# Graph layer, attention and a mixture of experts on one core: the experts' first layer in seven products for eight

## The chip, the core and the metric

The kernel runs on one core of a Trainium2 chip. TensorE multiplies matrices into eight banks of PSUM; VectorE, ScalarE and GpSimd do the rest of the arithmetic; SyncE (SP) and GpSimd issue the transfers. Each engine works through its own instructions in their order, and semaphores order the engines among each other. The metric is the device time of one execution in microseconds (us). Before the change the median of three runs is 1558.56 us (1558.55 to 1558.76).

## The reference

`x` is 4096 tokens of 256 numbers, `adj` a 4096 x 4096 matrix of weights. All is float32.

```
f = layernorm(x)
x = x + concat(f, adj @ (f @ neigh_W.T) / (adj.sum(1) + 1)) @ lin_W.T
z = layernorm(x)                      # then a transformer block on z
z1 = z + attention(rmsnorm(z)) @ wo.T           # causal, 4 heads, 2 of keys
flat = rmsnorm(z1)
weights = the two largest of softmax(flat @ router_w.T), normalised
for e in range(8):                              # the experts
    hh = silu(flat @ w1[e].T) * (flat @ w3[e].T)        # 682 wide
    out = out + weights[:, e:e+1] * (hh @ w2[e].T)
result = x + z1 + out
```

Only an expert's own tokens (two experts for each token) have weights that aren't zero, so the kernel computes only those.

## The kernel before

The program has three stages on one core. The first (to about 533 us) is the product with `adj`, in seven products for eight (Strassen's scheme in Winograd's form: 2 x 2 blocks, sums of blocks ahead, sums of products behind). The second (to about 1044 us) is the attention; while it runs, each token's row is scattered into the lists of its two experts in memory. The third, from 1044 us on, is the experts, and the change lies in it.

**Groups.** An expert's list is cut into groups of 256 rows (whole groups, numbers 0 to 24) and a rest in groups of 128 rows (small groups, 25 to 41; 42 to 45 are rare and run only if the lists need them). `TURNS` gives the order: a place k in it (0 to 41) has group `TURNS[k]`. Places 0 to 8 are whole groups; after them small and whole ones are mixed by their share, and the last `LAST` places are whole groups.

**One group.** `load13` brings w1 and w3 of the group's expert (128 x 2 x 1408 numbers; blocks of 128 outputs, w1 and w3 in turn, and a last block that holds the 42 left-over rows of both), `load2` brings w2, `load_rows` the rows. Weights have five buffers, so they come four to five places ahead. `prepare` transposes the rows on TensorE into a bank and ScalarE copies them, scaled, to `xT`. `hidden` (L1457) is the first layer: for each pair of blocks, 128 x 128 weights stay in the array and 256 (small group: 128) columns of `xT` pass, two products for the two halves of the 256 inputs (L1476); ScalarE takes silu of one bank (L1482) and VectorE multiplies it with the other bank (L1483). These banks come from three pools of two banks each in turn (`p_sc`). `combine` is the second layer. For a small group it is six products with 256 columns (L1528) into a bank `y`, which VectorE scales (L1543). For whole groups from place 4 on (`SEVEN`) it is seven products for eight: `split` (L1412 to L1419) has VectorE make eight sums of 128 x 384, `seven_products` (L1440) fills banks `y` and `ms`, VectorE adds the products up (L1447 to L1454) and ScalarE scales (L1539). Each half of a group is then scattered by GpSimd with addition into a buffer in memory (L1548).

**The order.** The order of all instructions is written by hand. For place k it is: `hidden(k)`, in it `prepare(k+1)` and at its end `split(k)`; the load of w13 for place k+5; `combine(k-1)`; the loads of rows and w2 for place k+4. So TensorE does a first layer, the transposes for the next group, then the second layer of the group before. VectorE has `split(k)` ahead of the scaling of place k-1, and that ahead of the multiplications of place k+1. `load_rows(k+4)` on SyncE waits until the scatter of place k-1 has landed, as it overwrites the row numbers that the scatter uses.

**The end.** Scatters of all but the last `LAST` groups add into `acc_dram`. Then one transfer copies that to the output (L1671), and the last groups' scatters add into the output itself, so they wait for the copy.

Of the kernel before, what the change touches and what calls it, by code (L numbers as in the profile page):

```python
# [9 lines left out]
F32 = mybir.dt.float32  # L10
I32 = mybir.dt.int32
SP = mybir.EngineType.SP
AF = mybir.ActivationFunctionType
ALU = mybir.AluOpType
# [3 lines left out]
P = 128  # L18
# [30 lines left out]


ALONE = 9
LAST = 5
RARE = 4
NM = NG - RARE
TURNS = list(range(ALONE)) + [
# [10 lines left out]
def fast_kernel(  # L66
# [596 lines left out]
    with (  # L663
# [1 line left out]
        tc.tile_pool(name="eg", bufs=1) as eg,  # L665
        tc.tile_pool(name="ex", bufs=2) as ex,
        tc.tile_pool(name="ax", bufs=2) as ax,
        tc.tile_pool(name="a_sc0", bufs=1, space=PSUM) as p_sc0,
        tc.tile_pool(name="a_sc1", bufs=2, space=PSUM) as p_sc1,
        tc.tile_pool(name="a_sc2", bufs=1, space=PSUM) as p_sc2,  # L670
        tc.tile_pool(name="a_y", bufs=1, space=PSUM) as p_y,
        tc.tile_pool(name="a_ms", bufs=1, space=PSUM) as p_ms,
    ):

        HALF = GR // P
        pt_all = sp.tile([P, 9 * 1024], F32, name="pt_all")
# [25 lines left out]
            given_back.update(keys)  # L702
            ring[:] = [r for r in ring if homes.get(id(r)) not in given_back]

        p_sc = cycle((p_sc0, p_sc2, p_sc1))
        p_sa = cycle((p_sc0, p_sc2))
        y_banks = [
            pool.tile([P, 512], F32, tag=tag, name=name) for pool, tag, name in (
# [662 lines left out]
        def prepare(k, pool=p_y, tag="y"):  # L1371
            i = TURNS[k]
            n = halves(i)
            tr = pool.tile([P, 2, n, P], F32, tag=tag, name=f"tx_{i}")
            for h in range(n):
                for c in range(2):
                    nc.tensor.transpose(  # L1377
                        tr[:, c, h, :], rows[i][:, h, c * P : (c + 1) * P], ident
                    )
            xT = late[:, LATE_XT + k % 2 * 2 * GR : LATE_XT + k % 2 * 2 * GR + 2 * n * P]  # L1380
            xT = xT.rearrange("p (c i) -> p c i", c=2)
            for c in range(2):
                nc.scalar.activation(  # L1383
                    xT[:, c, :], tr[:, c].rearrange("p h i -> p (h i)"), AF.Copy,
                    scale=ln2_sb[:, c : c + 1],
                )
            inputs_of[i] = xT

        SEVEN = [k for k in range(4, NM - 2) if TURNS[k] < NW]
        parts_of = {}

        def split(k, hT):

# [60 lines left out]
        def hidden(k, step=None, behind=None):  # L1457
# [4 lines left out]
            free_bank = k >= SEVEN[0]  # L1462

            for q in range(0, NF + 1, 2):
                pool = next(p_sc)
                if pool is p_sc1:
                    ps = [
                        pool.tile([P, 2, GR], F32, tag="sc", name=f"h_{i}_{q}_{m}")[:, :, 0:n]
                        for m in range(2)
                    ]  # L1470
                else:
                    ps = pool.tile([P, 2, 2, GR], F32, tag="sc", name=f"h_{i}_{q}")
                    ps = [ps[:, m, :, 0:n] for m in range(2)]
                for m in range(2 * q, min(2 * q + 4, 2 * NF + 1)):
                    for c in range(2):
                        nc.tensor.matmul(  # L1476
# [169 lines left out]
        def step():  # L1646
            for f in next(rest, []):
                f()

        load13(2)  # L1650
        load2(2)
        load13(3)
# [2 lines left out]
        for k in range(NM):  # L1655
            if k == NM - 1:


                between = iter([lambda: None, lambda: combine(k - 1)])
            hidden(  # L1660
                k, step if k < NM - 1 else lambda: next(between)(),
                k + 1 if k + 1 < NM else None,
            )
            step()
            if k + 5 < NM:
                load13(k + 5)
            if 0 < k < NM - 1:
                combine(k - 1)
                step()
            if k == NM - LAST:  # L1670
                nc.sync.dma_start(out, acc_dram[0:N, :])  # L1671
            if k + 4 < NM:
                load_rows(k + 4)
            if k + 4 < NM:
                load2(k + 4)
        combine(NM - 1)
    kv_scope.close()
    return lists

# [736 lines left out]
```

## Time and profile before

| | |
|---|---|
| median of three runs | 1558.56 us |
| profiled execution | 1558.78 us |
| its span | 1557.0 us |
| granted TensorE clock, mean | 0.999 |

The profile is of one execution, so its durations add up to 1558.78 us: the span and 1.8 us around it. Busy time by stage, from the trace (us):

| stretch | long | TensorE | VectorE | ScalarE | GpSimd | memory, GB/s |
|---|---|---|---|---|---|---|
| 0 to 533.4, product with `adj` | 533.4 | 528.1 | 379.6 | 53.5 | 290.2 | 140 |
| to 1043.7, attention | 510.3 | 509.0 | 418.6 | 302.3 | 235.1 | 37 |
| to 1187.7, places 0 to 9 | 144.0 | 144.0 | 83.2 | 38.7 | 43.4 | 240 |
| to 1472.1, whole and small groups mixed | 284.4 | 284.4 | 129.2 | 75.9 | 64.0 | 246 |
| to 1550, the last five first layers | 77.9 | 76.5 | 34.9 | 17.8 | 21.4 | 146 |

Lines of the profile have a start (or a total), a duration, the engine, the line of the code and what was written from what. PE is TensorE, PEld its loads of weights, DVE VectorE, ACT ScalarE, POOL GpSimd, SP SyncE. A float32 product of the program is two matrix instructions in the trace, so the 22 products of a first layer are x44. Matrix instructions overlap: the time that one takes in the stream is the distance of the starts, not the duration shown. In brackets stands how long the engine sat idle before, and what ended it.

### The profile page before, as it was taken

The numbers are of one execution on the slowest core, as the hardware profiler recorded it, in microseconds if no ns is written. First come the engines' busy times: TensorE is split into PE (matmuls) and PEld (weight loads), VectorE is DVE, ScalarE is ACT, GpSimd is POOL, SyncE is SP. The second block draws the span as 40 slices with busy tenths as digits, with TensorE's granted clock in tenths as the row PEclk, the third lists the DMA queues.
The fourth block names the chain that finished last, engine by engine and source line by source line (L and its number), as shares of the span: only waits on it lengthen the run. The fifth ranks groups of instructions, "written<-read, shape, count | busy, mean of one in ns | idle before, by whom it ended". The sixth has DMA issues, their size and how long they took to land.

```text
span 1557.0 us, 27444 instructions
## 1 busy us (share of the span) xinstructions
PE 1541.9 (99%) x10692; PEld 1133.8 (73%) x10692; DVE 1045.4 (67%) x2137; ACT 488.1 (31%) x884; POOL 655.0 (42%) x725
## 2 busy tenths in 40 slices
PE   8999999999999999999999999999999999999997
PEld 7888888888888643444444444358899999999996
DVE  7966677766766677779879878785565453544462
ACT  1101010010010356555665655652122222222221
POOL 3446557565565323364564553442422212122213
PEclk9999999999999999999999999999999999999999
DMA  6344444443444000011011011048677778777772
GB/s 236 129 129 146 139 139 135 139 139 136 139 136 142 32 1 16 29 36 51 29 57 33 29 39 37 22 184 314 192 229 207 228 249 264 232 242 246 237 232 29
DMA packets 68507, 209.34 MB, mean 134 GB/s; under 512 B 17488, under 2 KB 45520, under 8 KB 54736
## 3 DMA queue, kind: packets, MB, share of 16 engines
q1 hardware_dynamic: 55104, 189.50, 35.5%
q0 software_dynamic: 12720, 17.47, 5.8%
q8 instruction: 86, 1.41, 0.4%
q10 hardware_dynamic: 544, 0.52, 0.1%
q14 instruction: 53, 0.43, 0.1%
HBM read 184.48 MB, written 27.13 MB: 136 GB/s over the span
## 4 chain that ended last, share of the span: by engine, by line
PE 96%; DVE 2%; DMA 0%; POOL 0%; issue 0%; ACT 0%; SPq 0%; POOLq 0%; DVEq 0%; ACTq 0%
PE acc L493 25%; PE h L1476 21%; PE sc L757 14%; PE y_first L799 5%; PE y_second L799 5%; PE ye_y L1528 4%; PE y_third L799 4%; PE ye_y L1440 3%; PE ye_ms L1440 2%; PE pq L194 2%; PE ph L545 2%; PE pf L464 1%; PE po L876 1%; PE tx L1377 1%; PE trq L229 1%; PE tr L376 1%
## 5 line engine op out<-in xcount | busy, mean ns | idle before, releaser
L757 PE MATMUL sc<-qT_all,kT 64*64 64x512 f32 (+3 forms) x2304 | 282.0, 557 | 1.0 <-ACT pt_all L765 0.5
L493 PE MATMUL acc<-a,g 128*128 128x256 f32 x1024 | 245.9, 380 | 0.0
L1548 POOL DMA_INDIRECT acc_dram<-y,late x57 | 89.8, 1575 | 334.9 <-DVE y L1543 185.5
L493 PEld LDWEIGHTS acc<-a,g 128*128 128x128 f32 x1024 | 193.0, 190 | 31.6 <-DVE vv L511 1.2
L757 PEld LDWEIGHTS sc<-qT_all,kT 64*64 64x64 f32 x2304 | 91.2, 133 | 130.1 <-issue 108.2
L1483 DVE TENSOR_TENSOR late<-si,h 128x256 f32<-128x256 f32 (+2 forms) x126 | 62.7, 506 | 183.0 <-ACT si L1482 180.2
L765 ACT ACTIVATE pt_all<-sc 128x1024 f32<-128x1024 f32 (+3 forms) x157 | 149.0, 956 | 95.7 <-PE sc L757 95.1
L448 POOL TENSOR_TENSOR all_s<-all_s,more_sums 128x512 f32<-128x512 f32 x72 | 106.4, 1491 | 106.0 <-DVE more_sums L440 106.0
L1476 PE MATMUL h<-late,qT_all 128*128 128x256 f32 (+1 forms) x792 | 147.2, 345 | 0.0
L1482 ACT ACTIVATE si<-h 128x256 f32<-128x256 f32 (+2 forms) x126 | 57.0, 453 | 276.6 <-PE h L1476 269.4
L1476 PEld LDWEIGHTS h<-late,qT_all 128*128 128x128 f32 x792 | 130.1, 191 | 15.2 <-ACT late L1383 0.8
L493 PE MATMUL acc<-more_sums,g 128*128 128x256 f32 x512 | 126.2, 379 | 0.0
L785 DVE TENSOR_TENSOR late<-late,pt_all 128x1024 f32<-128x1024 f32 (+3 forms) x92 | 107.7, 1171 | 23.0 <-ACT pt_all L765 9.6
L1476 PE MATMUL h<-late,pt_all 128*128 128x128 f32 (+1 forms) x704 | 113.5, 321 | 0.0
L1476 PEld LDWEIGHTS h<-late,pt_all 128*128 128x128 f32 x704 | 103.5, 191 | 8.0
L493 PEld LDWEIGHTS acc<-more_sums,g 128*128 128x128 f32 x512 | 97.2, 190 | 14.8
L799 PE MATMUL y_second<-pt_all,vv 64*64 64x512 f32 (+3 forms) x440 | 105.0, 555 | 0.0
L799 PE MATMUL y_first<-pt_all,vv 64*64 64x512 f32 (+3 forms) x440 | 104.3, 553 | 0.0
L1035 POOL DMA_INDIRECT lists<-row,slots x64 | 90.2, 1410 | 18.0 <-issue 15.3
L799 PE MATMUL y_third<-pt_all,vv 64*64 64x512 f32 (+3 forms) x376 | 89.8, 557 | 0.0
L378 ACT COPY qT_all<-tr 128x512 f32<-128x512 f32 x30 | 16.2, 589 | 210.5 <-PE tr L376 210.4
L1476 PE MATMUL h<-late,res_all 128*128 128x256 f32 (+1 forms) x352 | 68.3, 353 | 0.0
(394 smaller groups left out, 2997.4 us busy)
## 6 DMA issues: line engine op xcount, KB each, us to landing
a<-in_adj_dram SPq DMA_DIRECT2D x64, 1024.0 KB
qT_all<-in_w_dram SPq DMA_DIRECT2D x18, 1408.0 KB
pt_all<-in_w_dram SPq DMA_DIRECT2D x16, 1408.0 KB
res_all<-in_w_dram SPq DMA_DIRECT2D x17, 768.0 KB
pt_all<-in_w_dram SPq DMA_DIRECT2D x16, 768.0 KB
res_all<-in_w_dram SPq DMA_DIRECT2D x8, 1408.0 KB
qT_all<-in_w_dram SPq DMA_DIRECT2D x9, 768.0 KB
late<-lists SPq DMA_DIRECT2D x25, 265.0 KB
```

The source lines that it names most:

```text
L448: nc.gpsimd.tensor_add(all_s[:, i], all_s[:, i], sums_at[n % 2][k])
L493: nc.tensor.matmul(acc[bank][:, at, :], g[jb][:, right, k, :], m[left][:, k, :], start=(jb == 0 and k == 0 and at == 0), stop=(jb == NB - ...
L757: nc.tensor.matmul(ps[k * HP : (k + 1) * HP, j, :w], kT[sb][hd, i * P + k * HP : i * P + (k + 1) * HP], qT[b][hd, p, off:], start=True, st ...
L765: nc.scalar.activation(pt[:, :, :w], ps[:, :, :w], AF.Exp, scale=HD ** -0.5)
L785: nc.vector.tensor_add(sums[b, p][:, :, off:], before[:, :, off:], pt[:, :, : 512 - off])
L799: nc.tensor.matmul(accs[b, p][k][hd, off:], vv[sb][some, i, hd], pt[some, j, : 512 - off], start=(s == order_of(b)[0]), stop=(s == order_o ...
L1035: put = nc.gpsimd.indirect_dma_start(out=lists[:, :], out_offset=bass.IndirectOffsetOnAxis(ap=chosen[b][:, k, t, :], axis=0), in_=flats[b] ...
L1440: nc.tensor.matmul(p[number], m[left][:, j, :], m[right][:, j, :], start=(n % 4 == 0 and j == 0), stop=(j == 2), skip_group_check=True,)
L1476: nc.tensor.matmul(ps[m % 2][:, m // 2 - q, :], w13_sb[:, c, m * P : (m + 1) * P], xT[:, c, :], start=(c == 0), stop=(c == 1),)
L1483: nc.vector.tensor_mul(hT[:, q : q + both, :], si[:, 0:both, :], ps[1][:, 0:both, :])
L1528: nc.tensor.matmul(ps[h if last else 0][:, h, :], hT[:, q, cols], w2_sb[:, q, :], start=(q == 0), stop=(q == NF),)
L1548: put = nc.gpsimd.indirect_dma_start(out=(acc_dram if k < NM - LAST else out)[:, :], out_offset=at, in_=y[:, h, :], in_offset=None, comput ...
```

## The change

- `LAST` goes from 5 to 3. Places 9 to 38 now have small and whole groups in turn (at three of them two small ones follow each other), and only the last three places are whole groups in a row. The copy to the output starts two places later.
- 14 whole groups, at the places 10, 12, 14, 17, 19, 21, 23, 26, 28, 30, 33, 35, 37 and 39 (`SPLIT13`), get their first layer in seven products for eight. The 2 x 2 blocks are w1 or w3 against the two halves of the inputs, and the two halves of the inputs against the two halves of the 256 rows. A block product is five products of 128 x 128 by 128 columns, one for each block of outputs. The tail (the last block) stays as it was.
- The four sums of the weights (128 x 640 each) are made by GpSimd (`sums13`), two places ahead, just after `hidden(k)` in the program and ahead of `combine(k-1)`'s scatter. The four sums of the inputs are made by VectorE at the end of `prepare` (`sums_x`), from the bank with the transposes.
- `hidden_seven` replaces `hidden` in these groups. It works in two parts, of four and of one block of outputs, each with three banks (A, D, B). Products are collected in the banks; between them ScalarE copies bank A (`s1`, `u2`) and bank D (`s5`) out, VectorE adds later banks to the copies, ScalarE takes silu of `s1` and `u2` in SBUF, and VectorE multiplies `u2` with `s5` and `s1` with the last bank A.
- The three pools of two banks are closed after the attention, and one pool of six single banks (`e_h`) is opened for all first layers. The plain `hidden` takes two of them a step.

```diff
--- before.py
+++ after.py
@@ -49,7 +49,7 @@
 ALONE = 9
-LAST = 5
+LAST = 3
 RARE = 4
 NM = NG - RARE
 TURNS = list(range(ALONE)) + [
@@ -665,12 +665,14 @@
         tc.tile_pool(name="eg", bufs=1) as eg,
         tc.tile_pool(name="ex", bufs=2) as ex,
         tc.tile_pool(name="ax", bufs=2) as ax,
-        tc.tile_pool(name="a_sc0", bufs=1, space=PSUM) as p_sc0,
-        tc.tile_pool(name="a_sc1", bufs=2, space=PSUM) as p_sc1,
-        tc.tile_pool(name="a_sc2", bufs=1, space=PSUM) as p_sc2,
         tc.tile_pool(name="a_y", bufs=1, space=PSUM) as p_y,
         tc.tile_pool(name="a_ms", bufs=1, space=PSUM) as p_ms,
     ):
+        sc_scope, ctx_h = ExitStack(), ExitStack()
+        p_sc0, p_sc1, p_sc2 = (
+            sc_scope.enter_context(tc.tile_pool(name=f"a_sc{n}", bufs=bufs, space=PSUM))
+            for n, bufs in ((0, 1), (1, 2), (2, 1))
+        )
         HALF = GR // P
         pt_all = sp.tile([P, 9 * 1024], F32, name="pt_all")
@@ -702,7 +704,6 @@
             given_back.update(keys)
             ring[:] = [r for r in ring if homes.get(id(r)) not in given_back]
-        p_sc = cycle((p_sc0, p_sc2, p_sc1))
         p_sa = cycle((p_sc0, p_sc2))
         y_banks = [
             pool.tile([P, 512], F32, tag=tag, name=name) for pool, tag, name in (
@@ -1385,12 +1386,172 @@
                     scale=ln2_sb[:, c : c + 1],
                 )
             inputs_of[i] = xT
+            if k in SPLIT13:
+                sums_x(k, tr)
         SEVEN = [k for k in range(4, NM - 2) if TURNS[k] < NW]
-        parts_of = {}
+        SPLIT13 = [k for k in SEVEN if k > ALONE]
+        parts_of, sums13_of = {}, {}
+        p_h = []
+        rooms13 = [
+            room.rearrange("p (s k i) -> p s k i", s=3, k=NF)
+            for room in (
+                sum_all[:, 0 : 3 * NF * P],
+                res_all[:, 2 * W13 + 2 * W2 : 2 * W13 + 2 * W2 + 3 * NF * P],
+            )
+        ]
+        def sums13(k):
+            if k not in SPLIT13:
+                return
+            chunks = w13s[k % 5][:, :, 0 : 2 * NF * P].rearrange(
+                "p c (k r i) -> p c r k i", r=2, i=P
+            )
+            m = {f"A{r + 1}{c + 1}": chunks[:, c, r] for r in range(2) for c in range(2)}
+            for n, name in enumerate(("S1", "S2", "S4")):
+                m[name] = rooms13[SPLIT13.index(k) % 2][:, n]
+            m["S3"] = m["A21"]
+            nc.gpsimd.tensor_add(m["S1"], m["A21"], m["A22"])
+            nc.gpsimd.tensor_sub(m["S2"], m["S1"], m["A11"])
+            nc.gpsimd.tensor_sub(m["S4"], m["A12"], m["S2"])
+            nc.gpsimd.tensor_sub(m["S3"], m["A11"], m["A21"])
+            sums13_of[k] = m
+        def sums_x(k, tr):
+            xT = inputs_of[TURNS[k]]
+            room = kT[6 + SPLIT13.index(k) % 2].rearrange("p (n i) -> p n i", n=4)
+            m = {f"T{n + 1}": room[:, n] for n in range(4)}
+            for c in range(2):
+                for h in range(2):
+                    m[f"B{c + 1}{h + 1}"] = xT[:, c, h * P : (h + 1) * P]
+            for dst, c, h, less in (
+                ("T1", 0, 1, "B11"), ("T2", 1, 1, "T1"), ("T3", 1, 1, "B12"), ("T4", 1, 0, "T2"),
+            ):
+                nc.vector.scalar_tensor_tensor(
+                    m[dst], tr[:, c, h, :], ln2_sb[:, c : c + 1], m[less],
+                    op0=ALU.mult, op1=ALU.subtract,
+                )
+            sums13_of[k].update(m)
+        def hidden_seven(k, step, behind):
+            i = TURNS[k]
+            m, xT, w13_sb = sums13_of.pop(k), inputs_of.pop(i), w13s[k % 5]
+            hT = hTs[k % 2]
+            room_x = (
+                qT_all[:, 2 * (2 * W13) + W2 :] if SPLIT13.index(k) % 2
+                else wqkv_sb.rearrange("p c w -> p (c w)")[:, 0:1024]
+            )
+            room_y = ax.tile([P, TB, ROW], F32, tag="row", name=f"hy_{i}")
+            room_y = room_y.rearrange("p t c -> p (t c)")
+            room_z = ax.tile([P, 512], F32, tag="yT0", name=f"hz_{i}")
+            class Part:
+                pass
+            parts = []
+            for n, (k0, k1) in enumerate(((0, NF - 1), (NF - 1, NF))):
+                q = Part()
+                q.chunks = range(k0, k1)
+                q.rows = slice(k0, k1)
+                q.A, q.D, q.B = (
+                    p_h[0].tile([P, 4, P], F32, tag="h", name=f"h{name}_{i}_{n}")
+                    for name in "ADB"
+                )
+                w = (k1 - k0) * P
+                rooms = (
+                    [room_x[:, 0:w], room_x[:, w : 2 * w], room_y[:, 0:w]]
+                    if n == 0 else [room_z[:, j * w : (j + 1) * w] for j in range(3)]
+                )
+                q.s1, q.u2, q.s5 = (
+                    r.rearrange("p (k i) -> p k i", i=P) for r in rooms
+                )
+                q.pair = (room_x if n == 0 else room_z)[:, 0 : 2 * w]
+                parts.append(q)
+            one, two = parts
+            def product(q, bank, left, right, first=False):
+                for n, c in enumerate(q.chunks):
+                    nc.tensor.matmul(
+                        bank[:, n, :], m[left][:, c, :], m[right],
+                        start=first and n == 0, stop=True, skip_group_check=True,
+                    )
+            def copied(dst, q, bank):
+                nc.scalar.copy(dst, bank[:, 0 : len(q.chunks), :])
+            def added(dst, q, bank):
+                nc.vector.tensor_add(dst, dst, bank[:, 0 : len(q.chunks), :])
+            def begun(q):
+                product(q, q.A, "A11", "B11", True)
+                copied(q.s1, q, q.A)
+                product(q, q.D, "S1", "T1", True)
+                copied(q.s5, q, q.D)
+                product(q, q.B, "A12", "B21", True)
+            def second(q):
+                product(q, q.A, "S2", "T2")
+                copied(q.u2, q, q.A)
+                product(q, q.D, "S4", "B22")
+            def added_up(q):
+                added(q.s1, q, q.B)
+                added(q.u2, q, q.D)
+            def third(q):
+                product(q, q.A, "S3", "T3")
+                added(q.s5, q, q.A)
+            def gated(q):
+                nc.scalar.activation(q.pair, q.pair, AF.Silu)
+            def last(q):
+                product(q, q.A, "A22", "T4")
+            def multiplied(q):
+                nc.vector.tensor_mul(hT[:, q.rows, P:GR], q.u2, q.s5)
+                nc.vector.tensor_mul(
+                    hT[:, q.rows, 0:P], q.s1, q.A[:, 0 : len(q.chunks), :]
+                )
+            begun(one)
+            second(one)
+            added_up(one)
+            step()
+            begun(two)
+            tail = two.B[:, 2:4, :].rearrange("p k i -> p (k i)")
+            for c in range(2):
+                nc.tensor.matmul(
+                    tail, w13_sb[:, c, 2 * NF * P :], xT[:, c, :],
+                    start=False, stop=(c == 1), skip_group_check=True,
+                )
+            second(two)
+            added_up(two)
+            gated(one)
+            third(one)
+            third(two)
+            step()
+            if behind is not None:
+                prepare(behind, p_ms, "ms")
+            gated(two)
+            si = ax.tile([P, GR], F32, tag="rden", name=f"si_{i}_t")
+            nc.scalar.activation(si[T0 : T0 + TAIL, :], tail[0:TAIL, :], AF.Silu)
+            last(one)
+            last(two)
+            multiplied(one)
+            multiplied(two)
+            nc.vector.tensor_mul(
+                hT[T0 : T0 + TAIL, NF, :], si[T0 : T0 + TAIL, :], tail[T0 : T0 + TAIL, :]
+            )
+            hidden_of[i] = hT
+            split(k, hT)
         def split(k, hT):
@@ -1462,15 +1623,10 @@
             free_bank = k >= SEVEN[0]
             for q in range(0, NF + 1, 2):
-                pool = next(p_sc)
-                if pool is p_sc1:
-                    ps = [
-                        pool.tile([P, 2, GR], F32, tag="sc", name=f"h_{i}_{q}_{m}")[:, :, 0:n]
-                        for m in range(2)
-                    ]
-                else:
-                    ps = pool.tile([P, 2, 2, GR], F32, tag="sc", name=f"h_{i}_{q}")
-                    ps = [ps[:, m, :, 0:n] for m in range(2)]
+                ps = [
+                    p_h[0].tile([P, 2, GR], F32, tag="h", name=f"h_{i}_{q}_{m}")[:, :, 0:n]
+                    for m in range(2)
+                ]
                 for m in range(2 * q, min(2 * q + 4, 2 * NF + 1)):
                     for c in range(2):
                         nc.tensor.matmul(
@@ -1647,6 +1803,8 @@
             for f in next(rest, []):
                 f()
+        sc_scope.close()
+        p_h.append(ctx_h.enter_context(tc.tile_pool(name="e_h", bufs=6, space=PSUM)))
         load13(2)
         load2(2)
         load13(3)
@@ -1657,11 +1815,15 @@
                 between = iter([lambda: None, lambda: combine(k - 1)])
-            hidden(
-                k, step if k < NM - 1 else lambda: next(between)(),
-                k + 1 if k + 1 < NM else None,
-            )
+            if k in SPLIT13:
+                hidden_seven(k, step, k + 1)
+            else:
+                hidden(
+                    k, step if k < NM - 1 else lambda: next(between)(),
+                    k + 1 if k + 1 < NM else None,
+                )
             step()
+            sums13(k + 2)
             if k + 5 < NM:
                 load13(k + 5)
             if 0 < k < NM - 1:
@@ -1674,6 +1836,7 @@
             if k + 4 < NM:
                 load2(k + 4)
         combine(NM - 1)
+        ctx_h.close()
     kv_scope.close()
     return lists
```

## The prediction

> **What bounds it now.** I read the page's busy shares and its chain of work that ended last, then that chain from 1290 to 1345 us, then the timeline of all engines there, then the first stage for what GpSimd does to VectorE.
>
> ```profile
> PE 1541.9 (99%) x10692; PEld 1133.8 (73%) x10692; DVE 1045.4 (67%) x2137; ACT 488.1 (31%) x884; POOL 655.0 (42%) x725
> ...
> PE 96%; DVE 2%; DMA 0%; POOL 0%; issue 0%; ACT 0%; SPq 0%; POOLq 0%; DVEq 0%; ACTq 0%
> ```
>
> TensorE sets the end; the other engines have room. In the chain, a whole group (x44 at 9.50) and a small one (x44 at 4.91) follow each other without a gap:
>
> ```profile
> 1305.01 4.91 PE h L1476 x44
> 1309.92 0.44 PE tx L1377 x4
> 1310.36 2.68 PE ye_y L1440 x24
> 1313.04 2.01 PE ye_ms L1440 x18
> 1315.05 9.50 PE h L1476 x44
> 1324.55 0.22 PE tx L1377 x2
> 1324.77 2.59 PE ye_y L1528 x12
> 1327.36 4.91 PE h L1476 x44
> ```
>
> So a change gains what it takes from TensorE's stream and loses every wait that it puts into it. The timeline shows the waits that are now just covered:
>
> ```profile
> 1303.56 0.56 DVE L1412 TENSOR_TENSOR kT<-late 128x384 f32<-128x384 f32 x1
> ...
> 1308.44 0.48 DVE L1543 TENSOR_SCALAR y<-ye_y,gt 128x256 f32<-128x256 f32 x1
> ...
> 1310.19 1.50 PE L1440 MATMUL ye_y<-qT_all,late 128*128 128x128 f32 x12
> ...
> 1315.09 0.29 DVE L1451 TENSOR_TENSOR vv<-vv,ye_ms 128x128 f32<-128x128 f32 x1 [0.78 <-PE ye_ms L1440]
> ...
> 1315.73 1.03 ACT L1539 ACTIVATE y<-vv,gt 128x256 f32<-128x256 f32 x2 [2.39 <-DVE vv L1452]
> ...
> 1318.39 1.57 POOL L1548 DMA_INDIRECT acc_dram<-y,late  x1 [0.19 <-issue]
> ```
>
> VectorE frees bank y at 1308.92, TensorE writes it again at 1310.19: 1.27 us of slack. L1451 starts 0.21 after TensorE's last product at 1314.88: that is TensorE to VectorE. ScalarE to TensorE is 0.06 (its L765 ends 535.63, sc goes on at 535.69), VectorE to TensorE 0.10 (first L174 done at 549.80, transposes at 549.90).
>
> **The products.** One product is two instructions. 44 long ones run from 1314.88 to 1324.38, 0.2159 each; 44 short ones from 1327.19 to 1332.11, and the 42 of L1440 in 4.69, 0.1117 each. Of a whole group's 44 long ones 40 go (8.64 us) and 70 short ones come (7.82); the tail's 4 stay (0.86). Saved: 0.82 a group, 14 groups, **-11.4 us**. The ratio 0.1117 : 0.2159 is 0.52, under the 4 : 7 at which seven for eight breaks even.
>
> [...] L1440's 42 back-to-back instructions decide for 0.1117.
>
> **The new chain in a whole group.** I set t = 0 at its first product and lay the new order out; a short product is 0.223. First and second round of the four-chunk part end at 4.46, the one-chunk part's first at 5.13, the tail at 6.00, its second at 6.44, the third round at 7.34 and 7.56, transposes of the small group behind (x2, 0.22) at 7.78. Each product into a used bank waits for its reader. The copies (128x512, 0.59 as L378; 128x128, 0.27 as L1447) are queued on ScalarE behind L1539 of the group before, which ends at t = 1.88: they end at 2.47 and 3.06, where TensorE wants the banks at 2.68 and 3.57. Covered, by 0.15 in the first case; if the cover went, 0.1 to 0.3 a group.
>
> Not covered is the last product, A22 T4, which adds to bank A after VectorE has read the third round from it: 7.34 + 0.21 + 0.69 (128x512 with one input in a bank, as L1483) + 0.10 = 8.34, against 7.78. **A wait of 0.56 in 13 groups; 0.34 in the last**, with four transposes behind: +7.6 us. Bounds: 0.4 to 0.7 each. The last products end at 9.45 instead of 9.72.
>
> **GpSimd's sums.** Four of 128x640. By L448 (512 wide, 1.26) and L453 (256 wide, 0.73) one is 1.53, four 6.1; bounds 1.45 to 1.8 each, as these are strided and depend on one another. Their data is early: that weight load was issued over 20 us before. In GpSimd's queue they stand behind the two scatters of the group before last (the second at 1318.39, done by t = 5.1) and ahead of the next scatter, whose y comes at t = 16 or later: it isn't delayed, nor SyncE's loads that wait for it. But GpSimd holds VectorE:
>
> ```profile
> 78.68 1.58 POOL L448 TENSOR_TENSOR all_s<-all_s,more_sums 128x512 f32<-128x512 f32 x1 [5.85 <-DVE more_sums L440]
> 79.73 0.69 DVE L469 TENSOR_TENSOR res_all<-res_all,pf 128x512 f32<-128x512 f32 x1 [0.60 <-PE pf L464]
> ```
> ```profile
> 112.26 1.26 POOL L448 TENSOR_TENSOR all_s<-all_s,qT_all 128x512 f32<-128x512 f32 x1
> 112.39 0.36 DVE L161 BATCH_NORM_AGGREGATE mv<-st 128x2 f32<-128x6 f32 x4
> 112.67 1.40 DVE L438 TENSOR_TENSOR more_sums<-a 128x512 f32<-128x512 f32 x1
> ```
>
> L469, one input in a bank, keeps its 0.69. L438, both in SBUF, takes 1.40 instead of 0.69: it ends 0.55 after the GpSimd operation. At a boundary of two such operations VectorE gets in and GpSimd waits (the pair at 117.35 takes 3.01, not 2.5).
>
> The sums run from t = 5.1: 6.7, 8.2, 9.7, 11.3. The adds from banks pass. The product of gate and copy (u2 with s5, both in SBUF) is due at 8.56, its silu long done (128x1024, 1.02 as L765, from 6.7), and is held to 9.7, done 10.3, and pushes the fourth sum to 11.8; its one-chunk twin is held to that, done 11.9; then 0.3 and 0.42 (tail): the split starts at 12.7 instead of 11.15 (now 11.0). Split 4.46 and y's 0.90 by the rows: bank y free at 18.08 (without the hold 16.55). TensorE wants it at 9.45 + 2.59 + 4.91 + 0.44 = 17.39. With the 0.10, **a new wait of 0.79**; without the hold none. VectorE's four sums of the inputs (0.29 each as L1448) then end level with the need for bank ms: 0.1 more. This happens where the group two before is whole and the one two after is one of the 14: places 10, 12, 19, 21, 28, 35, 37, seven times: +6.2 us. Elsewhere the sums fall earlier or there are none. Bounds: 0 (VectorE slips through) to 1.5 each.
>
> **The end.** The copy of the sums to the output now starts two groups later, behind the scatter of place 38. From the first product of place 39: y at 16.55, scatter 0.29 on, copy 6.23 after it (1488.75 to 1494.98), so 23.1. By its row (first scatter behind it 1511.11) it holds GpSimd for 16.1, to 39.2. Of the six scatters then left the last starts 2.1 + 4 x 1.87 later (as from 1511.11 and 1518.24), at 48.8. TensorE alone would set it to 9.45 + 2.59 + 9.94 + 4.69 + 19.87 (place 41 with its two second layers) + 0.96 to the scatter (1548.40 to 1549.36), 47.5: +1.3. Bounds: 0 (the copy shares the queues with no load now) to 2.7 (y's buffer waits for place 39's scatters to land).
>
> Six banks in a row instead of three pools: a hidden layer still gets each bank back after three steps, now in halves. The first ones take over banks that the unload leaves at 1046.48, wanted at 1048.76: nothing; if all six waited for that, 2.8. VectorE's and ScalarE's added work has room apart from the waits named.
>
> **Sum:** -11.4 + 7.6 + 6.2 + 1.3 = +3.7 on 1558.8; the median is 0.2 lower: **1562.3**. A difference under 0.2% (3.1 us) can't be told from none.
>
> **Rivals.**
> - As forecast, 1559.5 to 1566: 44%. Some two thirds of it is slower by over 0.2%.
> - GpSimd's sums don't reach TensorE: -11.4 + 7.6 and 0 to 1.3 for the end, 1555 to 1556. Not slower. It decides from the point where VectorE loses under 0.7 us a group to the sums: bank y's slack of 17.39 - 16.55. For it: only two of VectorE's operations before the split have both inputs in SBUF. Against it: 112.67. 24%.
> - The wait before the last product is hidden too: 1547 to 1552. It takes a read of bank A done in 0.4 us, which no row shows. 13%.
> - The sums are slower (1.8 and more each), or two waits push one another on: 7 x 1.5 and a wait of 0.7, 1567 to 1575. 19%.
> - Short products that are no cheaper: no room for it beside L1440's rows.
>
> The range takes in all but the best of the third and the worst of the fourth: 1551 to 1570. Faster by over 0.2%: all of the third (13%) and 13 of the second's 24; within: the other 11 of it and 15 of the first's 44, 26%; slower: 29 of the first and all of the fourth, 48%.
>
> **What would show it.** Right: in a whole group 70 short instructions in 7.8 us; TensorE idle some 0.5 us before the last round, released by VectorE's add; idle again before the seven products of the second layer in seven groups, released by L1543's like; VectorE's SBUF product at over 1 us beside GpSimd's sums. Wrong: no idle in TensorE's row, or idle at the first copies, at the inputs' sums, or where the stages meet.

## The result and the profile after

The changed kernel takes 1571.49 us (median of 6 runs, 1568.12 to 1574.74) beside 1558.55 of the kernel before on the same chip (6 runs, 1558.19 to 1558.76). The ratio is 1.0083, with a 95% interval of 1.007 to 1.0096: slower by some 13 us, where 3.7 had been forecast. The runs of the kernel before lie within 0.6 us, those after within 6.6. The profiled execution took 1571.55, with a span of 1569.7 (before: 1558.78 and 1557.0), so 12.7 us of span are to be found.

The page's busy shares and the shares of its chain by engine come first.

```profile
PE 1541.1 (98%) x11112; PEld 1141.3 (73%) x11112; DVE 1116.1 (71%) x2291; ACT 516.9 (33%) x954; POOL 746.4 (48%) x781
...
PE 87%; DVE 9%; ACT 1%; issue 1%; DMA 1%; POOL 1%; SPq 0%; DVEq 0%; ACTq 0%; POOLq 0%
```

VectorE now holds 9% of the chain, 2% before, so new waits lie on the path. TensorE counts as busy as long as before (1541.1 beside 1541.9), though 14 x 0.82 us of products went: the lengths of its instructions cover part of a wait (below, a wait that costs 0.60 is listed with 0.34), and some ran at a clock of 0.50 (1047.97 to 1051.39, below). The list of what TensorE waited for (total, times, longest) names them. None of these lines is in the list of the kernel before.

```profile
PE hA L1481 <- DVE hy L1490: 4.5, 13, 0.4
PE h L1632 <- DVE yT L809: 2.8, 1, 2.8
PE ye_ms L1601 <- DVE pick L1664: 2.5, 8, 0.8
...
PE ye_y L1601 <- DVE y L1699: 1.2, 3, 0.4
PE sc L758 <- DVE res_all L552: 1.1, 1, 1.1
```

The first line is the wait that the prediction priced. The second and fifth lie where the stages meet, where it priced nothing and which it had named as a sign of being wrong. The third is for bank ms, the fourth for bank y; the prediction had put nearly all of the sums' loss on bank y.

To see what each costs, I cut both traces at the same places: the experts' first product, the start of place 10 (the first group in seven products), the end of TensorE's last product, and the end of the span.

| us | before | after | difference |
|---|---|---|---|
| start to the experts' first product | 1043.67 | 1047.11 | +3.44 |
| from there to place 10 | 144.03 | 147.54 | +3.51 |
| place 10 to TensorE's end | 360.86 | 364.39 | +3.53 |
| TensorE's end to the end of the span | 8.44 | 10.66 | +2.22 |

The four add up to 12.7. More than half lies ahead of place 10, before any product of the new kind runs. The timeline around the experts' first product shows the first row:

```profile
1044.70 1.75 DVE L786 TENSOR_TENSOR sum_all<-sum_all,res_all 128x256 f32<-128x256 f32 x2
1046.38 0.68 DVE L809 TENSOR_TENSOR yT<-yT,y_second 128x512 f32<-128x512 f32 x1
1047.11 5.41 PE L1632 MATMUL h<-late,qT_all 128*128 128x256 f32 x16 [2.80 <-DVE yT L809]
```

TensorE stands still for 2.8 us until VectorE has read the last values from y_second. The sixteen instructions behind take 5.41 us where sixteen of 0.2159 take 3.5. The stretches of half a microsecond say why; the third number from the end is the granted clock (then follow the DMA share and GB/s):

```profile
1047.50:1048.00 0.50, 0.50 (x4) 0.45 (x3) 0.00 (x0) 0.50 (x1) 0.00 (x0) 0.97 0.95 356
1048.00:1048.50 0.50, 0.50 (x3) 0.41 (x2) 0.00 (x0) 0.41 (x1) 0.00 (x0) 0.50 1.03 387
...
1051.00:1051.50 0.50, 0.50 (x3) 0.38 (x3) 0.00 (x0) 0.00 (x0) 0.00 (x0) 0.61 1.13 457
1051.50:1052.00 0.50, 0.50 (x4) 0.45 (x3) 0.00 (x0) 0.31 (x1) 0.00 (x0) 1.00 1.03 427
```

By the means of the first and third of these stretches the clock is at 0.50 from 1047.97 to 1051.39: 3.42 us at half speed, 1.7 us lost. The rest of the second row (1.8) is at places 8 and 9, where the first sums on GpSimd run.

In a whole group the chain of waits now reads like this, in the stretch that the prediction showed for the kernel before:

```profile
1301.24 0.70 DVE hy L1490
1301.98 1.17 PE hA L1481 x8
1303.18 0.69 DVE late L1520
...
1304.96 1.14 DVE kT L1573
...
1313.11 0.87 DVE kT L1436 x3
1314.12 2.25 PE ye_ms L1601 x18
```

VectorE's add of the third round (L1490) stands ahead of the last products, as forecast. Then the chain stays on VectorE: gate by value and the split (its first operation at 1.14 where 0.56 is its length without company). From 1310.51 it passes VectorE's first multiplication of the small group, two silu and the copies of the inputs on ScalarE, and goes back to VectorE for the sums of the inputs from bank ms; the second layer gets bank ms 0.14 us after the last of them.

### The profile page after: what moved, and what is told of

Its sections match the earlier page's. It is cut to its first block, busy times and chain, and to the rows that moved or that the text cites. A ratio compares the mean times of both kernels' runs of the same rounds, so it can differ in the third digit from the quotient of the medians.

```text
span 1569.7 us, 28703 instructions
## 1 busy us (share of the span) xinstructions
PE 1541.1 (98%) x11112; PEld 1141.3 (73%) x11112; DVE 1116.1 (71%) x2291; ACT 516.9 (33%) x954; POOL 746.4 (48%) x781
## 4 chain that ended last, share of the span: by engine, by line
PE 87%; DVE 9%; ACT 1%; issue 1%; DMA 1%; POOL 1%; SPq 0%; DVEq 0%; ACTq 0%; POOLq 0%
PE acc L493 24%; PE sc L758 14%; PE h L1632 10%; PE y_second L800 5%; PE y_third L800 4%; PE y_first L800 4%; PE hA L1481 4%; PE ye_y L1684 3%; PE ye_ms L1601 2%; PE pq L194 2%; PE hD L1481 2%; PE ph L545 2%; DVE sum_all L786 1%; PE po L877 1%; PE ye_y L1601 1%; PE pf L464 1%
## 5 line engine op out<-in xcount | busy, mean ns | idle before, releaser
L1704 POOL DMA_INDIRECT acc_dram<-y,late x61 | 95.6, 1568 | 275.7 <-DVE y L1699 167.0
L1638 ACT ACTIVATE si<-h 128x256 f32<-128x256 f32 (+2 forms) x84 | 34.9, 417 | 204.2 <-PE h L1632 182.1
L1632 PE MATMUL h<-late,qT_all 128*128 128x128 f32 (+1 forms) x572 | 96.0, 327 | 2.8 <-DVE yT L809 2.8
L1632 PEld LDWEIGHTS h<-late,qT_all 128*128 128x128 f32 x572 | 86.4, 193 | 11.9 <-DVE yT L809 3.7
L1639 DVE TENSOR_TENSOR late<-si,h 128x256 f32<-128x256 f32 (+2 forms) x84 | 37.4, 460 | 69.3 <-PE h L1632 35.3
L768 POOL TENSOR_SCALAR_AFFINE_SELECT pt_all<-pt_all 128x256 f32<-128x256 f32 x36 | 20.6, 574 | 107.5 <-ACT pt_all L766 79.8
L493 PE MATMUL acc<-qT_all,g 128*128 128x256 f32 x256 | 65.7, 379 | 0.0
L1632 PE MATMUL h<-late,pt_all 128*128 128x128 f32 (+1 forms) x440 | 64.8, 306 | 0.0
```

Source lines behind the costliest of these rows:

```text
L493: nc.tensor.matmul(acc[bank][:, at, :], g[jb][:, right, k, :], m[left][:, k, :], start=(jb == 0 and k == 0 and at == 0), stop=(jb == NB - ...
L1632: nc.tensor.matmul(ps[m % 2][:, m // 2 - q, :], w13_sb[:, c, m * P : (m + 1) * P], xT[:, c, :], start=(c == 0), stop=(c == 1),)
L1704: put = nc.gpsimd.indirect_dma_start(out=(acc_dram if k < NM - LAST else out)[:, :], out_offset=at, in_=y[:, h, :], in_offset=None, comput ...
```

## The experiments

The theory I began with (A): the loss is where the stages meet, 5 to 6 us; at places 8 and 9 and the end, 1.8 and 2.2; the rest is what was forecast. The rival (B): GpSimd's sums and the waits that they push on one another make most of it, and the banks nothing. The first two kernels do one part of the change alone; the next two take one part out. The chips differ a little: the kernel before took 1558.04 to 1558.55 beside these runs, so differences between runs on two chips are good to some 0.4 us.

**The banks alone.** `LAST = 5` again and `SPLIT13 = []`: no product, sum or order of the change is left, only the PSUM pools.

> The new PSUM layout alone: the six banks in a row, with the two other pools opened first, as in the changed kernel; no first layer in seven products, no sums on GpSimd, and the order and the end of the kernel before. Theory A (the loss comes from where the stages meet): 5.1 to 5.7 us slower than before, 1563.6 to 1564.3. Of it 1.1 us is the first scores, late on TensorE at 533; 2.9 is the first product of the experts at 1044, waiting for the unload's add on VectorE; 1.7 is a granted clock near 0.5 to 0.9 in the 6 us behind that idle time. Theory B (GpSimd's sums and the waits they push on one another cost it, and the banks nothing): 1558.5, same as before. Theory C (the wait at 1044 is there, but the low clock is chance): 1562.5, and a clock of 1.00 behind the wait.

1563.93 us beside 1558.16, ratio 1.0037 (1.0023 to 1.005): +5.8, as A has it. The wait is the same 2.8. In the profiled execution (1562.62, the shortest of five) the clock stays at 1.00 behind it (the sixteen instructions take 3.72, not 5.41), and place 10 comes 144.04 after the first product, as in the kernel before; the other four took 1563.76 to 1564.22. These have no trace; they are 1.1 to 1.6 us longer, about what the low clock costs, and three of the four have a mean clock of 0.997 (the traced one 0.998). By these figures the low clock seems to come in most runs, not all: C is half right, and the experiments with idle products below take it up.

**The end alone.** `LAST = 3` in the kernel before.

> The kernel before with one edit, LAST = 3 in place of 5: three whole groups at the end, so other places for the whole groups between small ones, and the copy of the sums to the output issued two places later. Theory A: 2.2 us slower, 1560.8, all of it behind TensorE's last product (10.8 us from there to the end in place of 8.6). Theory B: 0 to 1.3 us slower, 1558.6 to 1559.9, since the changed kernel's own late work makes the rest of its end.

1559.94, ratio 1.0012 (1.0003 to 1.0021): +1.8, between A's 2.2 and B's 1.3. From place 10 to TensorE's end it takes 360.86, as before to the hundredth: the other order of the groups costs nothing. From there to the end 10.03 in place of 8.44. The copy is issued at 1521.59, the first scatter behind it runs at 1537.38, and six scatters are left. In the changed kernel:

```profile
1550.92 1.56 POOL L1704 DMA_INDIRECT out_dram<-y,late  x1 [0.19 <-issue]
1555.51 1.56 POOL L1704 DMA_INDIRECT out_dram<-y,late  x1 [2.91 <-DVE pick L1664]
```

Two scatters of a group are 1.87 apart, but from one group to the next it is 4.6, not 1.87.

**The banks taken over late.** In the changed kernel the three old pools serve until place 9, the six banks are opened ahead of place 10, and the scores begin with the other pool:

```
-        p_sa = cycle((p_sc0, p_sc2))
+        p_sa = cycle((p_sc2, p_sc0))
...
+            if k == ALONE + 1:
+                sc_scope.close()
+                p_h.append(ctx_h.enter_context(tc.tile_pool(name="e_h", bufs=6, space=PSUM)))
```

> The changed kernel, but the three old pools serve the first ten hidden layers as before, the six banks in a row are opened only ahead of place 10, and the first scores go to the two banks that no late read of the stage ahead holds. Theory A: the waits at 533 and 1044 and the low clock behind the second are gone, 5.7 us faster than the changed kernel, 1565.8. Theory B: no difference, 1571.5. If all six banks still wait for all three old pools, that wait moves to place 10, where the second layer of place 8 (4.7 us of TensorE) lies over it.

1567.67, ratio 1.0063 (1.0049 to 1.0076): 3.8 faster than the changed kernel, not 5.7. Up to place 10 it did what A says (1189.31 in place of 1194.65, 5.3 earlier, both waits and the low clock gone). But from there it took 365.97 in this execution, 1.6 more than the changed kernel, with the same instructions: 2.5 us of waits for bank y in place of 1.2. What the sums cost differs from run to run.

**Without GpSimd's sums.** Blocks of the weights stand where their sums would (`m.update(S1=m["A11"], S2=m["A12"], S4=m["A22"])`).

> The changed kernel without GpSimd's four sums of weights: blocks of the weights themselves stand in their place, so the hidden values of the 14 groups are other numbers; every product, copy and add is still issued. Theory A: only the loss around places 8 and 9 (1.8 us) and the three waits for bank y (1.6) go, so 3 to 4 us faster than the changed kernel, 1567.5 to 1568.5. Theory B: the sums are most of the loss, 8 us and more go, 1563.5 or less.

1563.32, ratio 1.0036 (1.0022 to 1.0049): 8.2 faster than the changed kernel. Here the part of A that made the sums small fell, and B's number came. Places 8 and 9 give back 1.8, as expected; but from place 10 to TensorE's end it takes 357.92 in place of 364.39, 6.5 less. The waits for bank ms are gone as well as those for bank y. I had put them down to the sums of the inputs, which are still there: they wait in VectorE's queue behind operations that can take longer while a sum runs (the same one 2.07 us in one place and 0.68 in another, below). Place by place, all 6.5 lies in the ten small groups that follow a whole one: six times 0.34 to 0.37, four times 0.8 to 1.2.

So both theories hold, each for its part: banks 5.8, end 1.8, GpSimd's sums 8.2, and the products with their own wait 2.9 gained (357.92 against 360.86). Together +12.9, the whole difference. The parts are not strictly apart, though: taken out of the changed kernel the banks gave back 3.8, not 5.8.

**Where the sums may stand.** In a whole group VectorE's work has both inputs in SBUF from the product of gate and copy to the end of the split. In a small one it reads banks. So the next kernel issues the sums behind the small group's scatter, on top of the late banks:

```
+            if TURNS[k] >= NW:
                 sums13(k + 2)
...
                 combine(k - 1)
                 step()
+            if TURNS[k] < NW:
+                sums13(k + 2)
```

> The kernel with the six banks opened late (1567.7), and GpSimd's sums for the whole group two places on issued behind the small group's scatter instead of ahead of it, some 14 us later, where VectorE reads banks. Theory A (the sums cost what they hold of VectorE's operations with both inputs in SBUF, the product of gate and copy and the split): the loss at places 8 and 9 and the ten of 0.35 to 1.2 us behind it go, 8.2 us faster, 1559.5. Theory B (sums hold VectorE wherever they stand, or come too late for their products): 2 us faster at most, 1565.7 or more, with waits of TensorE for the sums themselves or for bank ms.

1557.46, ratio 0.9996 (0.9987 to 1.0004): 10.2 faster than with the late banks alone, and 11 runs within 0.8 us. From place 10 on it takes 357.93, the same as with no sums. VectorE's rows in it:

```profile
1292.38 0.68 DVE L1520 TENSOR_TENSOR late<-wqkv_sb,hy 128x512 f32<-128x512 f32 x1
...
1301.67 2.13 POOL L1420 TENSOR_TENSOR res_all<-qT_all 128x640 f32<-128x640 f32 x1
1302.71 0.35 DVE L1437 SCALAR_TENSOR_TENSOR kT<-tx,ln_sb,late 128x128 f32<-128x128 f32 x1 [0.55 <-ACT late L1385]
```

(Line numbers are each kernel's own; here they are one higher.) The operations with two inputs in SBUF have their own lengths again (0.68, and 0.56 in the split), and the sum at 1301.67 lies beside operations on banks, which keep theirs (0.35 at 1302.71, as at 1290.22 in the changed kernel, where no sum runs). The gain is 2 more than expected. Of this 1.6 is loss of the same kind that the kernel it is compared with carried beyond the changed kernel's.

**The wait before the last products.** The one-chunk part and the tail move between the rounds of the four-chunk part: `begun(one)`, `begun(two)`, `second(one)`, `second(two)`, `third(one)`, `third(two)`, tail, transposes, `last(one)`, `last(two)`. The late banks are in, the sums where the change has them.

> The kernel with the six banks opened late (1567.7), and in a whole group the one-chunk part and the tail laid between the rounds of the four-chunk part, so that 1.5 us of TensorE's work instead of 0.6 stands between the third round and the last products. Theory A (the wait before the last products is VectorE's add of 0.69 and nothing else): all 13 waits of 0.5 go, 6.5 to 7.2 us faster, 1560.5 to 1561.2. Theory B (VectorE is behind anyway): the wait comes back at the second layer's banks, which are now wanted 0.5 us earlier: 3 us faster at most, 1564.7 or more.

1565.59, ratio 1.0038 (1.0025 to 1.0051), runs from 1560.84 to 1566.86: 2.1 faster, which is B. All 13 waits are gone, but in the profiled execution (1565.91) the second layer waits 5.6 us for bank y in 5 places and 3.5 for bank ms in 10, and behind the longest of these waits (2.2) the clock falls once (from 1382.94 six short products take 1.27, elsewhere 0.67). So in this execution what is taken from one wait goes to the next: ahead of that wait, beside the sums, two operations of the split take 1.23 and 1.77 where 0.56 is usual. Two of the five runs, 1560.84 and 1562.06, came close to A's number; they have no trace.

> Both edits in one kernel: the six banks opened late, the other order of the parts, the sums behind the small group's scatter. Theory A (the losses are apart and add up): 15 us faster than with the late banks alone, 1552.5 to 1553, and so 5 us under the kernel before, though the end still has its 1.8. Theory B (one wait covers the other): 1556 or more.

Both edits: 1551.07, ratio 0.9955 (0.9942 to 0.9968), 7.0 under the kernel before, with runs from 1548.74 to 1554.57. A, and some 1.5 more, with two new waits for sums, of 2.3 us and 0.4. The longer one:

```profile
1441.60 0.48 DVE L1706 TENSOR_SCALAR y<-ye_y,gt 128x256 f32<-128x256 f32 x1 [0.21 <-PE h L1639]
...
1447.94 1.55 POOL L1711 DMA_INDIRECT acc_dram<-y,late  x1 [9.17 <-PE ye_ms L1602]
1448.94 2.11 POOL L1420 TENSOR_TENSOR res_all<-qT_all 128x640 f32<-128x640 f32 x1
1451.11 1.16 PE L1482 MATMUL hD<-kT,res_all 128*128 128x128 f32 x8 [2.30 <-POOL res_all L1420]
```

The small group's y is ready at 1442.08; its scatter goes out at 1447.94, and the sums, queued behind it, are late for the product. The releaser that the line names was not the last: the scatter ahead was issued at 1436.71, and the table of transfers has 9.9 us as the median from issue to landing of the scatters between 1425 and 1465.

**All of it, with the old end.** The last kernel and `LAST = 5`.

> The same as the kernel with both edits, and LAST = 5 as in the kernel before: the copy to the output two places earlier, but three of the 14 groups in a row at the end. Theory A: the 1.8 of the end goes, 1551. Theory B: the three in a row, whose sums stand ahead of the scatters of the group before, lose it again: 1553 or more.

1565.43, ratio 1.0048 (1.0036 to 1.006): B, and far more than it asked. The end is back at 8.38. But TensorE waits 4.9 us for the first sum at place 30, 2.1 and 3.3 for VectorE and ScalarE at places 38 and 39, and each time the clock falls, behind the wait or late in it (0.51 in the three microseconds after the first; ten short products take 2.13 from 1492.93 and eight 1.84 from 1507.04, where 1.12 and 0.89 are usual). The three places take 6.8, 4.0 and 6.4 us more than the same work takes without a wait.

**The sums one group earlier.** They stay behind a scatter, four places ahead of their group (three where two small groups lie between): `if k == t - (3 if TURNS[t - 2] >= NW else 4): sums13(t)`, `LAST = 3`.

> The kernel with both edits (1551.1), and GpSimd's sums for a whole group issued one whole group earlier, still behind a scatter, so that they no longer stand behind a scatter that waits for the one before it to land (that scatter went out at 1447.94 for a y that was ready at 1442.1, and TensorE waited 2.3 us for the first sum). Theory A: both waits for sums, 2.7 us, go: 1548.4, and the runs lie within 1 us of one another. Theory B (the scatters, each some 10 us from issue to landing and each waiting for the one before, are behind by themselves and will hold something else): 1550.5 or more.

1549.42, ratio 0.9942 (0.9929 to 0.9956), five runs within 0.7 us: both waits for sums are gone, and the list of TensorE's waits has none in the experts. That is 9.0 us under the kernel before, and between A's 1548.4 and B's 1550.5, nearer to A. From place 10 to TensorE's end: 349.66, 11.2 less than before. The end takes 10.35, 1.9 more.

**Why the first product waits.** By the order in which the pools are opened, it writes a bank that the values' sums do not lie in (the trace has no bank numbers). The next kernel is the banks alone, but the pool with y_first and y_second stays open and serves as the third pair; only the four banks of the scores are taken over (`bufs=4`).

> The new PSUM layout alone (1563.9), but the pool that holds the values' sums stays open and serves as the third pair of banks; only the other four banks are taken over. Theory A (a pool opened on six banks waits for the last reader of any of them, so the first product waits for a bank that it doesn't use): the wait of 2.8 at 1044 and the low clock behind it go, 1558.2 to 1559.3, the upper end if the first scores are still late. Theory B (the first product waits for the unload's add in any layout that moves the two other pools): 1563 or more.

1558.52, ratio 1.0 (0.9991 to 1.0009). Nothing is left of the 5.8, and this is the row beside VectorE's:

```profile
1043.85 3.69 PE L1634 MATMUL h<-late,qT_all 128*128 128x256 f32 x16
```
```profile
1045.76 0.68 DVE L810 TENSOR_TENSOR yT<-yT,y_second 128x512 f32<-128x512 f32 x1
```

The first product starts 1.9 us ahead of the add that it waited for with six banks. So here a pool opened on the place of several waited for the last reader of all of them: 2.8 us with six banks, and no such wait with four. The late scores of 533 are gone in this layout too.

**Does the clock answer to the idle time?** The banks alone again, and in the wait products that nobody reads, into bank y.

> The new PSUM layout alone (1563.9, of which one run had no low clock, 1562.6, and four had a clock mean lower by 0.001, 1563.8 to 1564.2), and 12 products 256 wide that nobody reads in the 2.8 us in which TensorE waits; 2.6 us by 0.2159 each, so the wait itself ends as before. Theory A (the low clock answers to TensorE's idle time): the clock stays 1.00 behind it in every run, 1562.2 to 1562.7, within 0.7 us of one another. Theory B (it comes by chance whether TensorE is idle or not): 1563.9 and the same spread.

1564.7, ratio 1.004 (1.0026 to 1.0054). My size was wrong: a product is two instructions, so 12 took 5.3 us and held the first real one to 1050.07. Less those 2.4 it would be 1562.3, and the five runs lie within 0.5. Half as many:

> The run with idle products again, at the right size: a product is two instructions of 0.2159, so 12 products took 5.4 us and held the first real one 2.4 us longer than the wait. Now 6 products, 2.6 us, in the wait of 2.8. Theory A (the low clock answers to TensorE's idle time): the first product starts as with the layout alone, some 4 us later than in the kernel before, and every run keeps the clock: 1562.2 to 1562.7, within 0.7 us of one another. Theory B (the clock falls by chance in any case): 1563.9, with runs 1.6 apart.

1562.46, ratio 1.0025 (1.0016 to 1.0035), ten runs from 1562.02 to 1562.92, a little wider than A's 0.7. The wait is covered, the first product nearly as late as with the banks alone (1047.35 beside 1047.63), and in the traced execution the clock stays:

```profile
1044.49 2.86 PE L1821 MATMUL busy<-wo_sb,ident 128*128 128x256 f32 x12
1047.35 3.72 PE L1632 MATMUL h<-late,qT_all 128*128 128x256 f32 x16
```
```profile
1047.00:1049.00 2.00, 2.00 (x10) 1.47 (x9) 0.30 (x1) 1.28 (x1) 0.00 (x0) 1.00 1.00 395
```

1.5 us of the 5.8 are the clock's answer to an idle TensorE (1563.93 less 1562.46; 1.9 if each is first set against the kernel before on its own chip).

The traces show when the clock falls, and not all of why. In the changed kernel TensorE resumes at 1047.11, behind 2.8 us of idle time, and the clock is at 0.50 from 1047.97 on, for 3.41 us; without sums it resumes at 1046.94, behind 2.24, and the clock is low from 1047.25 on, for 3.41 again. In the changed kernel it falls once more, 4.3 us behind TensorE's last product, at 1563.39: 515.41 us after the first fall, 151 times the 3.413 that the first one lasted. Cut into steps of that length, counted from a fall, the 2.8 us of the changed kernel put 2.55 into the step that ends with the fall, 1044.56 to 1047.97, and no other step ahead of TensorE's end has more than 1.35. In the kernel before one step has 1.88 and doesn't end in a fall. So in these two traces a fall stands behind 2.55 us of idle time in one step, and none behind 1.88 or less. With the banks alone the same gap of 2.8 us, with the first product at 1047.63, left the clock at 1.00; how it lies in such steps isn't shown, and so not why.

## Why the prediction was wrong, step by step

- **The products: right.** With every wait gone 11.2 us are saved where the prediction had 11.4. A short instruction takes 0.1117 beside 0.2159 for a long one, a ratio of 0.52.
- **The wait before the last products: right.** A whole group's place takes 12.09 with it and 11.49 without: 0.60, forecast 0.56. (The list of waits has 0.34 for it.) With the sums out the net gain is 2.9, forecast 3.8.
- **The copies ahead of silu: right.** No wait for them in the changed kernel.
- **GpSimd's sums: right in kind, wrong in the places and the bank, 2 us short in all.** Forecast 6.2, measured 8.2. Between the profiled executions with and without the sums, the seven groups that I had counted lose 4.2, where I had 6.2. Three groups where I had written that the sums "fall earlier" (places 17, 26 and 33) lose 2.3. Places 8 and 9 (1.8), where the first sums fall into the split of place 8, were not counted at all. So the sum came near by luck: too much at five of the seven, and too few places. The loss also comes oftener through bank ms than through bank y, on which I had put 0.79 of 0.89 a group. A sum takes 1.54 to 2.14, not 1.53. And this is no even cost. At 1202.99 and at 1302.04 the same VectorE operation begins 0.01 us behind the start of the same sum; the first time it takes 2.07 and the sum 1.54, the second time it takes 0.68 and the sum 2.09:

```profile
1202.98 1.54 POOL L1421 TENSOR_TENSOR res_all<-res_all 128x640 f32<-128x640 f32 x1
1202.99 2.07 DVE L1519 TENSOR_TENSOR late<-wqkv_sb,hy 128x512 f32<-128x512 f32 x1
```
```profile
1302.03 2.09 POOL L1421 TENSOR_TENSOR res_all<-qT_all,res_all 128x640 f32<-128x640 f32 x1
1302.04 0.68 DVE L1519 TENSOR_TENSOR late<-wqkv_sb,hy 128x512 f32<-128x512 f32 x1
```

  Such ties may be one source of the spread of the runs (6.6 us, and 0.8 with the late banks and the sums moved), but that is not shown. The kernel without any sums still spreads over 3.5 us, with a wait of 2.2 and a low clock in its trace, and the one with both edits over 5.8, where the slowest run has the lowest mean clock (0.996).
- **The end: 1.3 forecast, 1.6 with `LAST` alone and 2.2 in the changed kernel.** The bound of 2.7 had the reason (a scatter waits for those ahead to land: 4.6 us between groups, where the sum had 1.87; the last group's, at 1561.91, has `[2.85 <-DMA out_dram<-y,late]`), and I took the lower value.
- **"Six banks in a row instead of three pools: … nothing; if all six waited for that, 2.8." This is the step that failed.** It compared the unload's end with the time at which the third pair of banks is wanted, since that pair holds the values' sums. All six waited, as the clause says and the four banks taken over instead show. Two things it did not have: the two other pools, opened first, moved the scores onto banks that the stage ahead still read (1.1 of wait at 533, 0.6 net in the profiled pair), and an idle time of 2.8 us costs up to 1.7 more through the clock. In all it is 5.1 in the profiled pair, 5.8 by medians, where the prediction had nothing.

With these put in (1562.3 + 5.1 + 2.0 + 0.9 for the end + 0.9 for the products) the forecast is 1571.2, beside 1571.49; it has to come near, since each correction is a measured one. The forecast of slower was right in its direction, but the larger part of the loss comes from what it had priced at nothing or too low, and the largest missing piece was in a clause at the end.

## What to carry to other kernels

When a change regroups banks, price the takeover for every bank by the last reader of any (2.8 us of wait here), and look at all places where a pool's position moved, not at the edited loop alone. Put GpSimd's two-input operations beside stretches in which VectorE reads banks (10.2 us here), and early enough to bear the scatters ahead of them in GpSimd's queue; until that is done, removing a wait elsewhere may gain little (2.1 of some 7 us here), because VectorE is late at the next one. And an idle time of TensorE can cost more than itself: behind 2.8 us the clock was at 0.50 for 3.42 in the changed kernel, 1.7 us more.

## What the runs showed of the hardware

- After 2.1 to 4.9 us without a product TensorE's granted clock fell in six of eight such places of the profiled executions. It was at 0.50 for 3.42 us in the changed kernel; in the run with the old end it was low for 6 us once, by the pace of the products (1507.04 to about 1513.1). Some falls came only after work had resumed, 0.3 and 0.9 us after it in the kernel without sums and in the changed one. After 2.8 us in the run with the banks alone, and 2.3 in the one with both edits, it stayed. Products that nobody reads, in the gap, kept the clock in both traces that have them (1.00 from 1044 to 1053 with six of them; with twelve, the sixteen instructions behind take 3.62).
- Where a VectorE operation with two inputs in SBUF began 0.01 us behind a GpSimd sum, either VectorE's took long (2.07 us, the sum 1.54) or the sum did (2.09, VectorE's 0.68). Which of the two it will be can't be told from the starts in the trace.
- Indirect scatters of 128 rows into the same tensor took 9.9 us to land (median between 1425 and 1465 in the run with both edits), 3.7 between 1300 and 1320 in the changed kernel, and 3.8 for its last six. The next group's waited for them: y ready at 1442.08, scatter at 1447.94. That the landing is what it waits for is read from the times and from other lines of the same kind (at 1561.91 in the changed kernel), not shown by an experiment of its own.
